# The front of an attention and expert kernel put in order by a greedy list, with sums per half and the scale folded into the joined weights

## The chip, the cores and the metric

The kernel runs on one core of a Trainium2 chip. The metric is the device time of one execution in microseconds (us). The engines are named as in the profile: PE (TensorE, matmuls), PEld (its weight loads), DVE (VectorE), ACT (ScalarE), POOL (GpSimd) and SP (SyncE, which issues nearly all DMAs). Each engine takes its instructions in the order of the program; semaphores let one engine wait for another.

## The reference

Cross attention, then a mixture of eight experts, on 16 batches of 112 tokens with 256 features. The context has 375 rows a batch.

```python
q = layernorm(x) @ Wq + bq;  k = ctx @ Wk + bk;  v = ctx @ Wv + bv
x = x + softmax(q @ k.T / 16) @ v
n = layernorm(x)
cw = softmax(n @ w_router) * softmax(10 * (n @ w_gating));  cw = cw / (sum(cw) + 1e-9)
x = x + sum over e of cw[e] * ((silu(n @ w_gate[e]) * (n @ w_up[e])) @ w_down[e])
```

w_gate and w_up are 8 x 256 x 1024, w_down is 8 x 1024 x 256. All is float32.

## The kernel before, in words

**Attention.** Wq and Wk are joined once into M = Wq Wk^T (turn_weights L190, join_weights L200), the biases into a column r, a row v and a scalar (join_biases L210, join_key_bias L220). Four batches are a group: attn_group (L233) makes the statistics of x on DVE, the power on POOL (L245), the normed x (xn, L251, DVE), its transposes, and qk = M xn + r. attn_batch (L284) is one batch in nine pieces: transposes of ctx and their copies (L293, L296), scores (L300), maximum and two small operations on DVE for the exp's bias (L305 to L309), exp with scale 1/16 (L313, ACT), transposes of p (L318), p times ctx (L327), its split into a high and a low part (L331, L332), projection by Wv in three passes (L337), x1 (L342), a DMA of x1 to the accumulator (L349), statistics of x1 (L353 to L357), the normed x1 (x1n, L360, DVE) and its transposes into x1T (L364, L366).

**Between.** The tokens are two halves of 8 batches. The expert matmuls are done in a seven-product scheme: four blocks of x and of a weight make seven sums each, and seven products replace eight. sums (L378) makes a batch's sums of x on DVE, each cast to a high part xs_hi on ACT (L375) and a low part xs_lo on POOL (L376). route (L394) makes the router's weights of a half.

**Experts.** 128 steps (expert, half, block of features, gate or up); step (L648) runs the seven products (prod, L567; 21 matmuls of 128x448), combines them on DVE (v1, w16, u3, c22, c21, c12) and fills PE in between with the down projection (down_group, L522). Weights come as raw pieces by DMA (L449), are turned into differences tt on POOL (L466 to L469), cast to a high part on ACT (L481) and a low part on POOL (L486). A plan (todo, from L496) says at which step each of this is due.

**Order.** Each engine's order in the front is written out by hand: generators for groups and batches are advanced tick by tick. A batch starts every two ticks, and within a tick the pieces go in a fixed sequence:

```python
    start = [max(0, 2 * b - 2) for b in range(B)]
    def tick(t, order=(3, 4, 2, 5, 6, 0, 1, 8, 7)):
        for s in order:
            for b in range(B):
                if t - start[b] == s == at[b]:
                    batch(b)
```

sums of a batch follow at start + 8 for the later four batches of each half. From tick T_STEP on, what remains of the front waits in a generator (rest), and steps 0 and 1 advance it at fixed points (offer). PSUM banks are taken in turn from a list of eight, of four from T_STEP on. SBUF buffers of the experts serve the front first: seven wide buffers hold x, ctx, qk, x1 and x1T, later the weights.

## Time and profile before

| | us |
|---|---|
| median of 3 runs (1002.86 to 1005.4) | 1004.77 |
| profiled execution | 1002.7 |
| its span, first to last instruction | 1000.9 |
| mean granted PE clock | 0.988 |

Times in the profile are us from the start of the span unless ns is said. In the windows view, PE busy is the time in which PE has a matmul; PEclk is the share of full speed that was granted. A wait line reads: engine, operation and line that waited, what ended the wait, total us, how often, longest.

| group of instructions (line) | count | mean ns |
|---|---|---|
| scores 128x375 on PE (L300) | 64 | 487 |
| exp 112x375 on ACT (L313), and reading its sum | 16 | 576 + 200 |
| normed x on DVE (L251) | 16 | 540 |
| normed x1 on DVE (L360) | 16 | 491 |
| small DVE operations for the exp's bias (L307, L309) | 32 | 214 |
| cast of sums, 128x112, on ACT (L375) | 40 | 280 |
| low part of sums, 128x112, on POOL (L376) | 40 | 450 |
| low part of a block of x, 128x448, on POOL (L376) | 4 | 1162 |
| low part of weights on POOL (L486) | 4 + 4 | 1005, 1322 |

The table holds 5 to 140 us. The ends of matmuls are modelled and overlap, so the time of a piece on PE is best read from start to start.

### The profile page before, as it was taken

The page shows a single profiled execution, that of the slowest core. Times are in us where ns is not written, and L with a number is a line of the kernel's source. Part 1 is how long each engine was busy: PE and PEld are TensorE (multiplying, and loading weights), DVE is VectorE, ACT ScalarE, POOL GpSimd, SP SyncE. Part 2 cuts the span into 40 slices and gives each one's busy share as a digit, 9 for nine tenths or more (in the row PEclk, how much of TensorE's full clock was granted, in tenths as well). Part 3 has the DMA queues.
Part 4 walks back from the last instruction along what each step waited for, and adds up shares of the span by engine and source line. Part 5 has one row for each costly group of instructions (what it writes and reads, how often), then busy time and mean ns, then how long its engine had stood idle before and what let it go on. Part 6 is the DMA issues. An engine that isn't in the chain of part 4 may idle for free.

```text
span 1000.9 us, 16367 instructions
## 1 busy us (share of the span) xinstructions
PE 980.1 (98%) x6052; PEld 911.3 (91%) x6052; DVE 802.8 (80%) x1529; ACT 496.4 (50%) x1036; POOL 419.0 (42%) x548
## 2 busy tenths in 40 slices
PE   8989889999999999999999999999999999999998
PEld 4868779999999999999999999999999999999998
DVE  5886668888878888878887887888887888788786
ACT  4555655445535554445544553555444544455342
POOL 2352765344605552356324460555235632455000
PEclk9999979999999999999999999999999999999999
DMA  9710111001100110011100110011001110010011
GB/s 216 213 30 16 53 32 53 16 28 44 53 1 23 43 43 22 12 42 37 39 11 22 44 54 1 22 44 43 22 11 43 44 32 11 22 43 2 1 37 38
DMA packets 36736, 39.06 MB, mean 39 GB/s; under 512 B 3552, under 2 KB 34656, under 8 KB 36656
## 3 DMA queue, kind: packets, MB, share of 16 engines
q1 hardware_dynamic: 36384, 37.76, 13.1%
q8 instruction: 47, 0.77, 0.3%
q10 hardware_dynamic: 272, 0.26, 0.1%
q14 instruction: 33, 0.27, 0.1%
HBM read 34.34 MB, written 1.84 MB: 36 GB/s over the span
## 4 chain that ended last, share of the span: by engine, by line
PE 93%; DVE 2%; DMA 2%; ACT 1%; POOL 1%; issue 0%; SPq 0%; DVEq 0%
PE pd L539 32%; PE pC L573 16%; PE pA L573 16%; PE pB L573 15%; PE pE L573 8%; PE ps_s L300 2%; PE ps_aT L327 1%; DMA wide<-in_x_dram 1%; PE ps_o L337 1%; PE ps_qk L271 1%; PE ps_lg L401 1%; DMA ctx<-in_ctx_dram 1%; PE ps_cT L293 1%; PE ps_pT L318 1%; ACT xs_hi L375 0%; POOL w L486 0%
## 5 line engine op out<-in xcount | busy, mean ns | idle before, releaser
L539 PE MATMUL pd<-wd,hhi 128*128 128x256 f32 x1792 | 338.6, 280 | 0.0
L539 PEld LDWEIGHTS pd<-wd,hhi 128*128 128x128 f32 x1792 | 310.1, 189 | 15.8
L539 PE MATMUL pd<-wd,hlo 128*128 128x256 f32 x896 | 251.9, 281 | 0.0
L573 PE MATMUL pC<-xs_hi,w 128*128 128x448 f32 x512 | 189.3, 370 | 0.8 <-DVE s_3c L702 0.8
L573 PE MATMUL pA<-xs_hi,w 128*128 128x448 f32 x512 | 188.6, 368 | 0.5 <-ACT v L674 0.4
L573 PE MATMUL pB<-xs_hi,w 128*128 128x448 f32 x512 | 187.9, 367 | 0.0
L539 PEld LDWEIGHTS pd<-wd,hlo 128*128 128x128 f32 x896 | 169.7, 189 | 0.2 <-DVE hlo L626 0.2
L556 POOL TENSOR_TENSOR acc<-acc,y 128x256 f32<-128x256 f32 x45 | 36.1, 831 | 248.4 <-ACT y L555 248.4
L486 POOL TENSOR_TENSOR w<-raw,w 128x384 fp32r<-128x384 f32 x64 | 73.0, 1141 | 136.8 <-ACT w L481 136.8
L674 ACT COPY v<-pA 128x448 f32<-128x448 f32 x128 | 68.1, 532 | 91.2 <-PE pA L573 91.2
L573 PEld LDWEIGHTS pC<-xs_hi,w 128*128 128x128 f32 x512 | 96.8, 189 | 10.0 <-DVE s_3c L702 1.1
L573 PEld LDWEIGHTS pA<-xs_hi,w 128*128 128x128 f32 x512 | 96.8, 189 | 6.0 <-ACT v L674 1.1
L573 PEld LDWEIGHTS pB<-xs_hi,w 128*128 128x128 f32 x512 | 97.2, 190 | 5.5
L573 PE MATMUL pC<-xs_lo,w 128*128 128x448 f32 x256 | 94.1, 368 | 0.0
L573 PE MATMUL pA<-xs_lo,w 128*128 128x448 f32 x256 | 94.1, 368 | 0.0
L573 PE MATMUL pE<-xs_hi,w 128*128 128x448 f32 x256 | 93.7, 366 | 0.0
L573 PE MATMUL pB<-xs_lo,w 128*128 128x448 f32 x256 | 93.3, 364 | 0.0
L486 POOL TENSOR_TENSOR w<-tt,w 128x512 fp32r<-128x512 f32 x64 | 82.9, 1296 | 2.6
L491 POOL TENSOR_TENSOR wd<-rawd,wd 128x512 fp32r<-128x512 f32 x32 | 41.8, 1307 | 72.7 <-ACT wd L490 72.7
L573 PEld LDWEIGHTS pE<-xs_hi,w 128*128 128x128 f32 x256 | 48.2, 188 | 3.9
L573 PEld LDWEIGHTS pB<-xs_lo,w 128*128 128x128 f32 x256 | 48.9, 191 | 1.9
L573 PEld LDWEIGHTS pC<-xs_lo,w 128*128 128x128 f32 x256 | 48.3, 189 | 2.3
(1779 smaller groups left out, 1884.4 us busy)
## 6 DMA issues: line engine op xcount, KB each, us to landing
raw<-in_L_ffn_w_gate_dram SPq DMA_DIRECT2D x32, 256.0 KB, 3.7
raw<-in_L_ffn_w_up_dram SPq DMA_DIRECT2D x32, 256.0 KB, 2.7
rawd<-in_L_ffn_w_down_dram SPq DMA_DIRECT2D x32, 256.0 KB, 2.8
ctx<-in_ctx_dram SPq DMA_DIRECT2D x13, 336.0 KB, 7.3
wide<-in_x_dram SPq DMA_DIRECT2D x4, 448.0 KB, 4.7
out_dram<-acc SPq DMA_DIRECT2D x6, 256.0 KB, 2.2
wide<-in_ctx_dram SPq DMA_DIRECT2D x3, 336.0 KB, 7.0
ctx<-in_ctx_dram SPq DMA_DIRECT2D x13, 39.0 KB
```

What stands on the lines that cost most here:

```text
L271: nc.tensor.matmul(ps, m_sb[:, k, m * P : (m + 1) * P], xnT[:, k, :], start=(k == 0), stop=(k == KC - 1),)
L293: nc.tensor.transpose(ps[:, c * KT : (c + 1) * KT], ct[:, c, k * P : (k + 1) * P], ident[:KT, :KT])
L300: nc.tensor.matmul(sc, qkT[g][:, k, i * TQ : (i + 1) * TQ], ctT[k], start=(k == 0), stop=(k == KC - 1),)
L318: nc.tensor.transpose(ps[:, c, :], p[:, c * KT : (c + 1) * KT], ident[:TQ, :TQ])
L327: nc.tensor.matmul(ps[:, k, :], ct[:, c, k * P : (k + 1) * P], pT[:, c, :], start=(c == 0), stop=(c == NK - 1),)
L337: nc.tensor.matmul(po, aT[:, a, k, :], (wv_hi, wv_lo)[w][:, k, :], start=(k == 0 and s == 0), stop=(k == KC - 1 and s == 2),)
L486: nc.gpsimd.tensor_sub(wts[k][1][:, d], w, f(wts[k][0][:, d]))
L491: nc.gpsimd.tensor_sub(t[:, 1], rawds[q], f(t[:, 0]))
L539: nc.tensor.matmul(pd, hs[a][:, t * P : (t + 1) * P], wds[q][w][:, fi, :], start=(opening and s == 0), stop=(last and s == 2), skip_group_ ...
L556: nc.gpsimd.tensor_add(acc[tt], acc[tt], y)
L573: nc.tensor.matmul(ps, w_[w][:, wi, :], (xs_hi, xs_lo)[a][h][xi], start=(start and s == 0), stop=(stop and s == 2), skip_group_check=True,)
L674: nc.scalar.copy(v1, pa)
```

## The change

The hand-written order goes. Every piece of the front becomes an operation of a list (class Line): engine, cost in us, priority, what it reads, writes and which buffers it takes. run() places them greedily: among the engines it takes the one that can begin first, and on it, of the pieces that could begin within 0.02 us, the one with the lowest priority number (mostly the batch's number). Buffers and PSUM banks come free when all their modelled uses have ended. Then all pieces are emitted in the order of their modelled begin.

```diff
+class Line:
+    LAG = {"PE": 0.2, "SP": 0.1}
...
+                t = max((end[d] + (0.0 if ops[d][0] == eng else self.LAG.get(ops[d][0], 0.1)) for d in deps), default=0.0)
...
+            for eng, c in ready.items():
+                at = max(free.get(eng, 0.0), min(x[0] for x in c))
+                x = min((x for x in c if x[0] <= at + 0.02), key=lambda x: (x[1], x[2]))
+                if best is None or at < best[0]:
+                    best = (at, eng, x)
...
+        for at, n in sorted(line):
+            ops[n][3]()
```

The loads: warm-up matmuls go from 8 to 11; ctx 0 is loaded before the bias rows, x of group 1 before Wv and ctx 2.

```diff
-    WARM = 8
+    WARM = 11
...
+        op("SP", 0.45, 4 * g - 6 if g else -22, lambda: load_x(g), new=(("xg", ("xg", g)),), kb=448)
...
+        op("SP", 0.85, b - 3.5, lambda: load_ctx(b), new=(("ctx", ("ctx", b)),), kb=375)
```

The scale 1/16 goes into M, r and v; the bias of the exp needs one small operation after a negated maximum, where there were two.

```diff
-            nc.scalar.copy(m_sb[:, i, :], ps)
+           lambda: nc.scalar.activation(m_sb[:, i, :], bank(k, [P, D]), AF.Copy, scale=SCALE),
...
-        nc.vector.reduce_max(mx, sc, axis=AX.X)
-        nc.vector.tensor_scalar(mx, mx, cb, None, op0=ALU.add)
-        nc.vector.tensor_scalar(nb, cb, mx, SCALE, op0=ALU.subtract, op1=ALU.mult)
-        nc.scalar.activation(p, sc, AF.Exp, bias=nb, scale=SCALE, accum_out=l)
+           lambda: nc.vector.reduce_max(top[:TQ, col], bank(("sc", b), [TQ, TK]), axis=AX.X, negate=True),
+           lambda: nc.vector.scalar_tensor_tensor(
+               low[:TQ, col], top[:TQ, col], cs[:TQ, col], cs[:TQ, col], op0=ALU.subtract, op1=ALU.add),
+               p(), bank(("sc", b), [TQ, TK]), AF.Exp, bias=low[:TQ, col], accum_out=total[:TQ, col]),
```

The normed x of a group is made on ACT (scale and bias from small columns), but for two of the four batches of group 0. The small per-batch tiles become columns of tiles that hold all batches.

The sums of x are made once a half, on 448 columns. Those of half 0 are in the list. Of half 1 only the two plain blocks X_A11 and X_A12 are; the rest is offered in steps 1 to 3:

```diff
-    def sums(b, eng):
+    def sum_x(h, i):
...
+        for i in (X_A11, X_A12):
+            split(h, i, (6.5, 28)[h], *early(h))
+    for n, i in enumerate((X_S1, X_S2, X_S3, X_S4)):
+        op("DVE", 0.63, 9.5 + 0.1 * n, lambda i=i: sum_x(0, i),
...
+    for i in (X_S2, X_S1, X_S3, X_A22, X_S4):
+        split(0, i, 10.5, *late(0), *([("sx", i)] if i != X_A22 else []))
...
+    def sums_later():
+        for i in (X_S1, X_S2, X_S3, X_S4):
+            sum_x(1, i)
+            yield
+        for i in (X_S2, X_S1, X_S3, X_A22, X_S4):
+            split_hi(1, i)
+            yield
+            split_lo(1, i, V if i in (X_S1, X_S2) else GP)
+            yield
```

The first three weight pieces (EARLY = 3), the first down weights, the whole of step 0 and the first product of step 1 are in the list too, with priorities after all batches. Step 0 takes its temporaries from buffers of the last batches, and its silu waits for every exp, those of both routers among them:

```diff
+    def P1(tag, i, start, stop, reads=(), fresh=False):
+        op("PE", 0.61, 30, lambda: first(tag, i, start, stop),
...
+    tail_s = [("ctT", b, k) for b in range(B - 3, B) for k in range(KC)]
+    P1("A", 1, True, False, fresh=True)
+    op("ACT", 0.54, 30, v1_, reads=(("first", "A"),), writes=("v1",),
+       waits=[("aT", B - 2), ("aTl", B - 2)])
+    P1("B", 6, True, True, fresh=True)
+    w16 = add("w", "v1", "B", "v1", ("first", "B"), waits=tail_s)
+    P1("C", 5, True, False, fresh=True)
+    P1("A", 2, False, True, reads=("v1",))
+    op("ACT", 1.9, 30, silu0, reads=(("first", "A"), "exp", w16), writes=("silu0",))
+    P1("E", 7, True, True, fresh=True)
...
+    op("PE", 0.61, 31, second, reads=(("w", 1), ("xs", 0, X_A11)), new=(("bank", ("second",), BANKS[4:]),))
...
+    line.run()
+    carry["silu01"] = lambda: silu(0, (0, 1), e0["c12"])
-    for n in range(len(steps)):
+    for n in range(1, len(steps)):
+        if n == 1:
+            waiting.append(sums_later())
         step(n)
```

Banks: the last two batches (from their scores on), the router of half 1 and the first product of step 1 may take only the four banks D0 to D3; step 0 takes A, B, C and E:

```diff
+        some = (BANKS[4:],) if b >= B - 2 else ()
...
+           new=(("bank", ("sc", b), *some),))
```

Steps from 2 on are as before.

## The prediction

> **What bounds the kernel now.** I read the page first: is one engine full, and does the chain that ended last stay on it?

> ```profile
> span 1000.9 us, 16367 instructions
> PE 980.1 (98%) x6052; PEld 911.3 (91%) x6052; DVE 802.8 (80%) x1529; ACT 496.4 (50%) x1036; POOL 419.0 (42%) x548
> PE 93%; DVE 2%; DMA 2%; ACT 1%; POOL 1%; issue 0%; SPq 0%; DVEq 0%
> ```

> TensorE (PE) is the bound, so only its idle time and its slow clock can be won back. The change touches the front (attention, until the expert steps run freely). So I cut the span into stages by the windows view:

> ```profile
> core 0: us, PE busy (x) PEld busy (x) DVE busy (x) ACT busy (x) POOL busy (x), PEclk, DMA share, GB/s
> 0.00:7.00 7.00, 3.98 (x12) 1.47 (x13) 2.11 (x9) 1.49 (x2) 0.70 (x6) 1.00 0.67 164
> 7.00:26.00 19.00, 17.16 (x82) 11.91 (x81) 13.43 (x45) 9.85 (x26) 7.00 (x8) 0.91 1.03 237
> 26.00:60.00 34.00, 34.00 (x231) 27.61 (x229) 26.62 (x97) 19.60 (x56) 14.43 (x22) 1.00 0.60 164
> 60.00:81.00 21.00, 16.91 (x119) 14.76 (x117) 15.71 (x56) 10.50 (x37) 11.58 (x23) 0.92 0.06 18
> 81.00:105.00 24.00, 24.00 (x163) 19.62 (x163) 16.03 (x59) 12.58 (x36) 6.55 (x13) 1.00 0.08 21
> 105.00:151.00 46.00, 38.25 (x188) 33.03 (x187) 30.39 (x75) 27.08 (x68) 34.65 (x55) 0.81 0.14 45
> 151.00:200.00 49.00, 49.00 (x303) 46.37 (x304) 41.52 (x69) 24.81 (x49) 19.63 (x25) 1.00 0.11 32
> ```

> The loss of a stage is idle time (length minus PE busy) plus clock (length times one minus PEclk). 7 to 26: 1.8 + 1.7. 60 to 81: 4.1 + 1.7. 105 to 151: 7.8 + 8.7. The others: none. Together 25.8 us, the most that a better order can win; from 151 us on PE is full. The causes are in the waits of PE up to 120 us and, for the end of the front, in PE's timeline:

> ```profile
> PE ps_pT L318 <- ACT p L313: 6.4, 5, 1.9
> PE ps_w L195 <- DMA wn<-in_L_xattn_Wq_dram: 1.8, 1, 1.8
> ```
> ```profile
> 120.27 1.16 PE L337 MATMUL ps_o<-wv_b,aT 128*112 128x256 f32 x6 [1.50 <-ACT aT L331]
> 128.24 0.60 PE L364 MATMUL ps_x1T<-ident,x1n 112*128 112x112 f32 x2 [2.92 <-DVE x1n L360]
> 129.79 5.99 PE L401 MATMUL ps_lg<-wr,wide 128*128 128x16 f32 x28
> ```

> ACT's timeline at 63 us shows the first cause: five casts xs_hi (L375) of one batch's sums stand ahead of the exp p (L313), and PE waits 1.6 us. The same happens at 70 and 108. At the end x1n (L360) of the last batch stands behind other work on DVE. After it the clock is 0.53 from 128 to 142.

> **What the change is worth, part by part.** The sum is made against the profiled execution (1002.7 us, span 1000.9); the median of the runs shown, 1004.77, lies 2.07 above it, and that is added at the end.

> *The list's costs.* Its order is good only if its costs are right. Against the trace: scores 1.33 (two back to back: 1.26 each), aT 1.35 (1.34), pT 0.33 (0.32), qk 1.51 (1.52), ctT copy 0.45 (0.473), exp 0.78 (0.576 + 0.200), split low 1.12 (1.162), weights low 1.02 and 1.31 (1.005, 1.322), batch statistics 0.8 (0.428 + 0.182 + 0.154). All within about 6%, and PE's own are rather high.

> *PE's work does not change.* A batch takes 4.46 us at full clock (92.20 to 96.65 in the timeline), 16 of them 71.4; a group 2 x 0.39 + 2 x 1.52 = 3.8, four 15.3; joined weights 0.9 + 1.75 + 0.87 = 3.5; router 14 x 0.42 = 5.9; step 0 and the next step's first product 24 x 0.205 = 4.9. Sum 101.0.

> *The other engines get lighter.* DVE: 16 scalar operations at 0.214 go with the folded scale (3.4 us); 14 of 16 norms at 0.54 go to ACT (7.6), against 4 small ones. No row shows this norm on ACT: between the 0.37 of a 128x256 copy and the 0.57 of a 128x448 cast I take 0.43, or 6.0 us on an engine that is half idle; the ends are 5.2 and 8.0, both covered. Sums per half: 8 batches x 5 casts of 0.28 become 10 of 0.567 (11.2 to 5.7 on ACT), the low parts 40 x 0.45 = 18 become at most 10 x 1.16 = 11.6, the sums 9.5 become 8 x 0.62 = 5.0; all of these lie beside PE. By the rows the front then needs about 84 us of DVE, 80 of ACT, 52 of POOL under PE's 101: covered, but at over 80% a queue can make PE wait.

> *Start (3.5 lost).* Three more warm-up matmuls at 0.445 end at about 6.1 where 4.75 was, so the gap before the first transposes (released by Wq at 6.58) falls from 1.84 to 0.5; I let nearly all of the clock's 1.7 go. On SP the first ctx now goes ahead of the bias rows and x of group 1 ahead of ctx 2. Chain of batch 0: x lands at 5.05, statistics 2.5, power 1.0, small ones 0.6, norms 0.9, transposes and copies 1.5, qk 3.0 and copy 0.6 give scores at 15.6 to 16.5 (now 18.6). Left: 1.5. Won: **2.0**. If ctx 2 comes late, 1 us of it is gone.

> *Middle (5.8 lost).* The casts get a later priority than the open batches and can run in the slack of ACT, so the wait behind L375 goes. Next in line is DVE. [...] The rows:

> ```profile
> L360 DVE TENSOR_SCALAR x1n<-wide,mvb,rsb x16: 399/406/1250, 34.4 to 127.7; 112x256 f32<-112x256 f32 x16
> L277 DVE CUSTOM_DVE_ANT_0 junk<-xn,mix x16: 416/424/2053, 15.0 to 89.7; 112x256 f32<-112x256 f32 x16
> ```

> Columns: count, shortest/median/longest ns. The lock is there (1.25 and 2.05 us where 0.41 is usual), but seldom: the means, 0.491 and 0.556, lie 0.09 and 0.13 above the medians. By the rows DVE's 84 us already hold this, and the middle keeps 2.0 of loss, most of it from order that doesn't fit to the tenth of a microsecond. [...] I take the row, because these long operations come late in the list. Left: 2.0. Won: **3.8**.

> *End of the front (16.5 lost).* From the last batch's scores to its x1T, by the rows: 1.3 + 0.54 + 0.2 + 0.78, then 0.33 + 0.44, 1.34 + 0.34 + 0.39, 0.75 + 0.48 + 0.76 + 0.56 + 0.41, 0.2 + 0.35, with 14 handovers of about 0.12: 10.9 us, of which PE works 3.9. To fill the other 7.0 PE has the rest of batch 14 (2.6), of 13 (1.0), router products (2.1) and the 24 products (4.9), together 10.6. So it can be filled, but not everywhere: batches 14 and 15 are held to four banks, of which the router's and the next step's product take one each, and step 0 waits for buffers that batches 13 to 15 set free. I leave 2.5 of idle time here.

> *New wait.* Step 0's silu now reads every exp, the router's of half 1 too. After the last x1T copy: two router products and drain 1.0, copy 0.25, maximum and subtraction 0.72, two exps 0.48, table load 1.28, silu 0.55, handovers 0.4: 4.7 us. In step 1 the multiply by that silu heads DVE's queue; behind it stand u3 and c22 (0.62 each), and PE's product into C needs c22. PE has five products meanwhile, to 3.9 us; c22 is there at 4.7 + 3 x 0.62 = 6.6. PE stands 2.7 us. Nothing in the traced order waits so long there (the multiply waited 0.54). In exchange two table loads of 1.28 on ACT are gone, which hid nothing and win nothing.

> *Clock.* [...] Here gaps of 1.63 and 1.92 (62.8 and 69.1) were followed by 0.5 from 72.9 to 76.1, and 1.50 plus 2.92 by 14 us at 0.53. [...] by the rows the 2.7 (and perhaps one before it) cost 1.7 each. I take the rows: 3.0. Left at the end: 2.5 + 2.7 + 3.0 = 8.2. Won: **8.3**.

> *Handed on.* The splits of half 1 that were made in the front (4 sums and 2 low parts on DVE, 6 x 0.62; 5 casts on ACT; 3 low parts on POOL) now lie in steps 1 to 3. A step takes 6.74 and holds 5.3 to 6.0 of DVE (windows from 164.7 to 178.3), so about 0.7 to 1.4 is free in each: 3.7 does not quite fit into three. Between 0 and 3; I take 1.3. POOL's early step holds 1.9 + 2.3 + 0.65 (weight differences, low parts, down weights) = 4.9 of 6.7 and takes its 3.5 over three steps. Copies of x1 to the accumulators (SP, behind each ctx load) and the raw weight loads, which now follow the last of them, land 2.7 to 3.7 us after issue, a whole step before use: nothing. Lost: **1.3**.

> Sum: 2.0 + 3.8 + 8.3 - 1.3 = 12.8. Profiled 1002.7 - 12.8 = 989.9; against the median 992.0.

> **Rivals.**
> A. The list fits as well as the stages with no loss at all: left are 1 at the start, 0.5 in the middle, 4 at the end. Won about 20: **985**. For it: 26 to 60 and 81 to 105 show a full PE under a fixed order. Against it: the silu wait.
> B. Won in front, given back in the steps: DVE in steps 1 to 3 costs the full 3 and the clock falls there once more or stays low as after 128 (up to 7). Won 3 to 7: **1000**.
> C. The list changes the order but its gaps are only elsewhere; every point won at the end is lost to banks: within 3 of before, **1004**.
> D. Slower. The engines keep a fixed order, and DVE, at 84 of 101, takes over as the bound: an x1n or a bias row behind a POOL operation delays a batch, and each such delay reaches PE. The price is what DVE needs beyond 101; it decides from 127 us on (101 plus the 25.8 now lost), that is when DVE's rows stretch 1.5 times. Batches that each lose 1.9 us, say, with the clock falling in between, give **1010**. Against it: means over medians show 6 us of such stops in the whole front, not 42.

> **How the numbers follow.** The sum's own case (won 8 to 17, 988 to 997): 0.50. A: 0.17. B: 0.15. C: 0.06. D: 0.12. A measurement of this kernel can tell about 0.3% (3 us) from no change; so faster 0.82, same 0.06, slower 0.12. For 8 in 10 the range goes to A's 984 below and to B's end, 1001.5, above; outside stay D, most of C and little beyond A.

> **What would show it.** Right: no clock under 1.0 between 7 and 26; PE full from 26 to about 100 with no wait for p behind xs_hi; the router's last products at about 112 rather than 135; a wait of PE for c22 of step 1 of 2 to 3 us; step 2 some 13 us earlier than now; from then on the same 6.74 per step. Wrong: waits of PE for x1n or nb in every batch (D), DVE full in steps 1 to 3 (B), or a PE that stands for a ctx load at the start.

## The result and the profile after

| | before | changed |
|---|---|---|
| median of 20 runs each (us) | 1003.97 (1001.46 to 1007.44) | 1007.69 (1006.48 to 1010.05) |
| ratio, 95% interval | | 1.0039 [1.0029, 1.0048] |
| profiled execution (us) | 1002.7 | 1007.49 |
| span of it (us) | 1000.9 | 1005.7 |
| mean granted PE clock | 0.988 | 0.993 |

The changed kernel is slower by 0.4%, where 992 us were forecast: 15.7 us above the forecast and outside the range. The page after, in the lines that were read first before:

```profile
span 1005.7 us, 16283 instructions
PE 981.5 (98%) x6055; PEld 911.1 (91%) x6055; DVE 807.0 (80%) x1481; ACT 497.9 (50%) x1017; POOL 416.0 (41%) x516
PE 91%; DVE 4%; DMA 2%; issue 1%; POOL 1%; ACT 0%; DVEq 0%; POOLq 0%; ACTq 0%
```

PE is still the bound, but DVE's share of the chain that ended last has doubled, from 2% to 4%. Fewer operations on DVE, and yet more time on the path. The windows view by the same stages, with one row for the steps added:

```profile
core 0: us, PE busy (x) PEld busy (x) DVE busy (x) ACT busy (x) POOL busy (x), PEclk, DMA share, GB/s
0.00:7.00 7.00, 5.47 (x17) 2.15 (x18) 2.21 (x10) 1.68 (x3) 0.70 (x6) 1.00 0.72 214
7.00:26.00 19.00, 17.19 (x93) 12.32 (x92) 13.85 (x52) 13.48 (x34) 9.65 (x11) 1.00 0.93 243
26.00:60.00 34.00, 31.93 (x205) 25.06 (x204) 25.05 (x78) 20.18 (x52) 11.66 (x14) 1.00 0.53 155
60.00:81.00 21.00, 16.35 (x121) 14.31 (x120) 17.48 (x40) 9.85 (x27) 14.78 (x20) 0.92 0.08 23
81.00:105.00 24.00, 21.50 (x142) 18.48 (x141) 15.73 (x42) 13.89 (x38) 10.06 (x13) 0.93 0.12 37
105.00:151.00 46.00, 39.73 (x222) 33.93 (x221) 34.08 (x75) 24.04 (x55) 21.03 (x27) 0.93 0.09 28
151.00:200.00 49.00, 47.76 (x295) 45.07 (x295) 42.31 (x67) 24.23 (x48) 23.13 (x27) 1.00 0.12 34
200.00:900.00 700.00, 700.00 (x4329) 663.23 (x4328) 573.30 (x978) 346.24 (x681) 305.89 (x378) 1.00 0.10 31
```

The start (7 to 26) has its clock back, and the end (105 to 151) is better: PEclk 0.93 instead of 0.81. The stages from 26 to 105, where PE was to be full, now lose idle time in each and clock in two. The last row hides something. The same row of before, in which PE is just as busy:

```profile
200.00:900.00 700.00, 700.00 (x4353) 664.34 (x4352) 577.67 (x985) 350.31 (x690) 307.80 (x381) 1.00 0.10 31
```

The 700 us are full in both, at full clock, and yet hold 24 matmuls fewer in the changed kernel (4329 instead of 4353): each step takes longer without any wait. "PE busy" can't show that; only counts, or starts of equal instructions, can.

To book both kinds of loss I counted, at each time, the elapsed time less the full-speed time of all PE work begun by then (each kind of matmul at its usual start-to-start time, the same in both kernels, the warm-up left out):

| stage, by the prediction's steps | lost before | lost after | won | forecast |
|---|---|---|---|---|
| start, to 26 us | 11.0 | 9.1 | 1.9 | 2.0 |
| middle, 26 to 105 | 5.9 | 12.7 | -6.8 | 3.8 |
| end of the front, 105 to 151 | 17.6 | 11.4 | 6.2 | 8.3 |
| handed on, 151 to 170 | 0.0 | 1.3 | -1.3 | -1.3 |
| steps, 170 to the end | -6.5 | -1.7 | -4.8 | 0 |
| sum | | | -4.8 | 12.8 |

At 170 us the two kernels stand level (34.5 lost in both): the start and the end have paid for the middle. The sum is the difference of the spans (-4.8). (The steps' losses are negative because the assumed matmul times are a little long; only their difference means something. With the median of each kind as its time the column of what was won reads 1.5, -6.4, 6.1, -1.2, -4.8: a stage is good to some 0.5 us.)

The middle's loss has a name. PE's waits between 5 and 155 us, longest first (us in total, times, longest):

```profile
PE ps_xx L950 <- DVE x1n L942: 7.7, 3, 4.5
PE pB L417 <- DVE s_1w L528: 2.7, 1, 2.7
PE ps_cT L846 <- DMA ctx<-in_ctx_dram: 1.2, 2, 1.0
```

The timeline at the longest (start, duration, then the instruction; in brackets the idle time before it and its releaser):

```profile
75.03 3.31 POOL L267 TENSOR_TENSOR xs_lo<-sx,xs_hi 128x448 fp32r<-128x448 f32 x3
75.09 4.49 DVE L942 TENSOR_SCALAR x1n<-wide,mv,rs 112x256 f32<-112x256 f32 x1 [0.44 <-POOL rs L936]
78.31 1.12 POOL L267 TENSOR_TENSOR xs_lo<-wide,xs_hi 128x448 fp32r<-128x448 f32 x1
79.64 0.64 PE L950 MATMUL ps_xx<-ident,x1n 112*128 112x112 f32 x2 [4.54 <-DVE x1n L942]
```

One pass over 112x256, whose median is 0.475 us, took 4.49. It began 0.06 us after a row of four low parts on POOL, and ended 0.15 us after the row did. Shortest, median and longest of the 16 passes, in ns:

```profile
L942 DVE TENSOR_SCALAR x1n<-wide,mv,rs x16: 403/475/4485, 31.1 to 123.4; 112x256 f32<-112x256 f32 x16
```

The second such place:

```profile
100.97 0.99 POOL L322 TENSOR_TENSOR w<-raw,w 128x384 fp32r<-128x384 f32 x1
101.03 3.25 DVE L942 TENSOR_SCALAR x1n<-wide,mv,rs 112x256 f32<-112x256 f32 x1 [0.44 <-POOL rs L936]
101.93 1.25 POOL L322 TENSOR_TENSOR w<-tt,w 128x512 fp32r<-128x512 f32 x1
103.15 0.98 POOL L322 TENSOR_TENSOR w<-raw,w 128x384 fp32r<-128x384 f32 x1
```

Each POOL operation begins before the one ahead has ended (101.93 is before 100.97 + 0.99): there is no gap in the row. (A third, at 52.1, took 2.33 us beside a row of two, and PE waited 0.6 us for it.) The clock was at a half from 77.5 to 84.4 and from 104.8 to 108.3.

A row without a gap in the records does not always hold the pass. In the same trace:

```profile
33.41 2.33 POOL L787 TENSOR_TENSOR wide<-wide,mix 112x256 f32<-112x256 f32 x3
33.47 0.81 DVE L942 TENSOR_SCALAR x1n<-wide,mv,rs 112x256 f32<-112x256 f32 x1 [0.67 <-POOL rs L936]
```

This row is of additions, each 0.72 us or more, and the x1n was through after the first of them (0.81 us); so was the one at 60.8. The experiments below are about rows of subtractions.

### The profile page after: what moved, and what is told of

It reads as the page before. It is cut to its first block, busy times and chain, and to the rows that moved or that the text cites. A ratio compares the mean times of both kernels' runs of the same rounds, so it can differ in the third digit from the quotient of the medians.

```text
span 1005.7 us, 16283 instructions
## 1 busy us (share of the span) xinstructions
PE 981.5 (98%) x6055; PEld 911.1 (91%) x6055; DVE 807.0 (80%) x1481; ACT 497.9 (50%) x1017; POOL 416.0 (41%) x516
## 3 DMA queue, kind: packets, MB, share of 16 engines
q1 hardware_dynamic: 36384, 37.76, 12.7%
HBM read 34.34 MB, written 1.84 MB: 36 GB/s over the span
## 4 chain that ended last, share of the span: by engine, by line
PE 91%; DVE 4%; DMA 2%; issue 1%; POOL 1%; ACT 0%; DVEq 0%; POOLq 0%; ACTq 0%
PE pd L383 31%; PE pC L417 15%; PE pA L417 15%; PE pB L417 15%; PE pE L417 7%; PE ps_aa L892 2%; PE ps_sc L858 2%; DMA ctx<-in_ctx_dram 1%; DVE x1n L942 1%; PE ps_po L907 1%; PE ps_cT L846 1%; PE ps_pp L879 0%; DMA wide<-in_x_dram 0%; PE ps_lg L978 0%; POOL rs L936 0%
## 5 line engine op out<-in xcount | busy, mean ns | idle before, releaser
L331 POOL TENSOR_TENSOR wd<-rawd,wd 128x512 fp32r<-128x512 f32 x32 | 42.1, 1316 | 68.5 <-ACT wd L329 68.4
```

The source lines that it names most:

```text
L331: nc.gpsimd.tensor_sub(wds[q][1], rawds[q], f(wds[q][0]))
```

## Experiments

Theories: (R) the list packs POOL's long operations back to back, and such a row holds an x1n on DVE for its whole length; (L) the lengthened step comes from where the buffers lie, since the eleven small column tiles (1472 bytes a partition; some expectations say twelve) moved the experts' buffers. Rivals: the loss lies in the new order itself (banks, the remainder of half 1 in steps 1 to 3), or one POOL operation is waited for at most. Ratios are to the kernel before, run on the same chip beside it. Its medians there lie between 1003.71 and 1004.97 us, so a difference in us between kernels of different experiments is good to about 1 us. A step's length is the median over a trace. Distances come from the addresses that the program was given.

**The kernel before once more**, unchanged, as a measure of the measurement.

> The kernel before, unchanged, to see how steady its steps are. In the traces at hand a step takes 6.74 us before and 6.79 after, with the same instructions. If that is a matter of the execution (rival theory: each execution draws its own rate), this profile may show any step between 6.73 and 6.80; if it belongs to the kernel, 6.74 again. Time: same as before, ratio 1.000.

1003.96 us, ratio 0.9996 [0.9982, 1.0011]; the step 6.74 us. So 0.3% is well resolved, and the step's length is a property of a program, not of a run.

**Column tiles moved behind the experts' buffers** in the changed kernel (another pool), so that these lie where they lay before.

```diff
-        return cpool.tile([P, *shape], F32, name=name)
+        return spool.tile([P, *shape], F32, tag=name, name=name, bufs=1)
```

> The changed kernel with the instructions in the same order, but its twelve small column tiles (1472 bytes a partition) lie behind the experts' buffers instead of ahead of them, so that those buffers lie where they lay before. Theory 'addresses': a step falls from 6.79 to 6.74 and the time by about 5 us, to 0.999 of before. Theory 'order of the program' or 'each execution its own': the step stays at 6.79, or anywhere, and the time at 1.004 of before.

1003.14 us, ratio 0.999 [0.9975, 1.0005]: 4.6 us less than the changed kernel. The step fell from 6.787 to 6.740 us; the waits for x1n stayed (7.6 us). Every engine's order is the same, so the step's length hangs on placement.

**A tile of 1472 bytes at the front of the pool of constants**, in the kernel before: it moves the constants, the blocks of x and the experts' buffers together.

```diff
+    pad = cpool.tile([P, 368], F32, name="pad")
...
-        lg = spool.tile([P, NTT, 2, E], F32, tag="lg", name=f"lg{h}", bufs=1)
+        lg = pad[:, : NTT * 2 * E].rearrange("p (j s e) -> p j s e", j=NTT, s=2)
```

> The kernel before with 1472 bytes more in the constant pool (the router's small tile is taken from them), so that the experts' buffers lie as in the changed kernel. Theory 'addresses': a step rises from 6.74 to 6.79, the time by about 5 us, ratio 1.005. Otherwise: step 6.74, ratio 1.000.

1003.25 us, ratio 0.9987 [0.9973, 1.0], step 6.740. The absolute addresses changed and the step didn't. The place of the experts' buffers alone, as my expectation had it, is thus not what counts; here the blocks of x moved along with them.

**x1n on ScalarE**, in the changed kernel, at the same place of the list:

```diff
-                t[0], x1(), mv1[:TQ, b, 0:1], rs1[:TQ, col], op0=ALU.subtract, op1=ALU.mult
+                nm1[:TQ, col], mv1[:TQ, b, 0:1], rs1[:TQ, col], -1.0, op0=ALU.mult, op1=ALU.mult
...
+            nc.scalar.activation(t[0], x1(), AF.Identity, bias=nm1[:TQ, col], scale=rs1[:TQ, col])
```

> The changed kernel with its list as it is, but each normed x1 is made on ACT (scale and a bias column from one small DVE operation) at the place where DVE made it. Theory 'lock': DVE's x1n waits for a whole row of POOL operations (4.49 and 3.25 us where 0.41 is usual); with it on ACT the waits of PE for x1n (7.7 us) and most of the slow clock behind them (about 3.4) go: about 10 us less than the changed kernel, 0.994 of before. Rival 'the list's order itself': x1n would come late anyway since it waits for the power on POOL and for ACT's queue: at most 2 us less.

1001.14 us, ratio 0.9963 [0.9954, 0.9973]: 6.5 us less than the changed kernel, where I expected about 10. The waits for x1n fell from 7.7 to 1.9 us (longest 0.8). Idle time from 60 to 105, by the windows: 3.1 + 0.03 instead of 4.65 + 2.5, and no clock below 1.00 there. Step 2 began at 126.7 us instead of 133.8. The step stayed at 6.787: the losses are separate. Of what is missing 1.7 us lie at the end: the clock was at a half for 6.8 us there (from 123.7) instead of 3.4. This speaks for R, but doesn't yet show that the row is the cause.

**An unused tile of 64 bytes behind the constants**, which moves only the experts' buffers: in the kernel before, and in the changed one.

```diff
+    pad = cpool.tile([P, 16], F32, name="pad")
```

> The kernel before with one unused tile of 64 bytes at the end of the constant pool: same instructions, the blocks of x stay where they are, the experts' buffers (weights, hidden blocks) move by 64 bytes. So far a step took 6.74 us where both lie at 64 above a multiple of 128 bytes (before, changed kernel with the small tiles moved) or both at a multiple of 128 (before with 1472 bytes ahead of everything), and 6.787 where x lies at 64 and the experts' buffers at 0 (the changed kernel, twice). Theory 'phase' (the two must share their place modulo 128): step 6.79, time 5 to 6 us more, ratio 1.005. Rival 'where exactly, or what else is in the constant pool': step 6.74, ratio 1.000.

> The changed kernel with one unused tile of 64 bytes at the end of its constant pool: same instructions in the same order, the experts' buffers move by 64 bytes more. Theory 'phase': step 6.74, time as with the small tiles moved, about 1003. Rival 'where exactly': step stays 6.787, time 1007.7.

Before with it: 1002.65 us, ratio 0.9982 [0.9971, 0.9993], step 6.720. Changed with it: 1003.25, ratio 0.999 [0.998, 1.0], step 6.740. The second came as expected; the first went the other way, which refuted my first rule (a period of 128 bytes). What fits all of these is the distance of the experts' buffers from the blocks of x modulo 256: 64 gives 6.787, 128 gives 6.740, 192 gives 6.720.

**Both repairs**: x1n on ScalarE and the columns behind the experts' buffers.

> The changed kernel with x1n on ACT in the same list and the small column tiles behind the experts' buffers. The two gains should add, since one is in the front and one in the steps: 1007.7 - 6.5 - 4.6 = 996.6, ratio 0.992. If the step's length depends on the order of the front, not on addresses, it stays at 1001.

996.81 us, ratio 0.9932 [0.9911, 0.9952]. The gains add.

**The same, with the sums of half 1 begun two offers later**, to take them from in front of step 1's combination.

```diff
     def sums_later():
+        yield
+        yield
```

> The same, and the sums of half 1 begin two offers later in step 1, so that DVE makes w16 of step 1 before them. PE waits 2.6 us for that w16 now; in DVE's queue ahead of it stand the router's last operations (2.0 us) and two sums (1.2 us). Theory 'sums ahead of w16': the wait falls by 1.2 us and with it perhaps the slow clock after it (6.8 us at half, 3.4 us): 1 to 4 us less, 993 to 995.5. Rival, my prediction's own: step 1 waits for silu behind the router's exps, then nothing changes.

997.46 us, ratio 0.9935 [0.9915, 0.9955]: no gain. The wait for s_1w fell from 2.6 to 1.4 us and step 2 began 4 us sooner (125.4), but PE then waited 0.8 us for s_1c and 1.9 for s_4c, and the clock was at a half from 124.0 to 134.2. At step 8 one of the 4 us was left (173.5 against 174.5). DVE owes these sums within three steps; moving them moves the wait.

**Single operations beside rows of 1, 2, 4 and 8 POOL subtractions**, in a small kernel that leaves the whole layer out.

> A kernel of its own (its output is a copy of x; nothing of attention or experts is computed). DVE, or ACT, makes one 112x256 operation that waits for a small POOL power; behind the power stand 0, 1, 2, 4 or 8 POOL subtractions of 128x448 in a row (about 1.1 us each). Theory 'lock for a whole row': a one-input DVE operation from SBUF (as x1n) takes 0.41 us alone and as long as the row lasts with it, about 1.2, 2.3, 4.5 and 9 us. Rival 'one instruction at a time': never more than 0.41 plus one subtraction, 1.5 us, however long the row. With two SBUF inputs the trace of the changed kernel shows 0.76 to 0.88 for a 0.62 us sum beside POOL, so an interleaving: at most one subtraction. From PSUM, and on ACT: no effect, 0.4 us for all.

The groups of DVE (mean ns after the comma):

```profile
L80 DVE TENSOR_SCALAR scalar_none<-xin,mean,r_scalar_none 112x256 f32<-112x256 f32 x3 | 1.2, 412 | 18.8 <-POOL r_scalar_none L69 18.8
...
L80 DVE TENSOR_SCALAR scalar_four<-xin,mean,r_scalar_four 112x256 f32<-112x256 f32 x3 | 3.6, 1208 | 3.7 <-POOL r_scalar_four L69 3.7
```

From 0.41 to 1.21 us, but no more beside four or eight than beside one; with two SBUF inputs 0.485 to 1.340; from PSUM (0.543), for the batch statistics (0.418) and on ScalarE (0.600) nothing. As it stood, this refuted R. But all subtractions of a row wrote one tile, and its timeline gives 4.74 us for four where each works 1.13: there was a gap of about 0.06 us between them, which the changed kernel's rows don't have.

**The same with a tile for each subtraction**, so that none depends on the one before. The tiles also have the type that the kernels use (fp32r), where the first had f32.

> As the first measurement of single operations beside rows of 1, 2, 4 and 8 GpSimd subtractions of 128x448 (it leaves the whole layer out; the output is a copy of x), with one difference: each subtraction of a row writes a tile of its own, in the type that the kernels use, so that none of a row depends on the one before. The theory 'a row without a gap holds VectorE for its whole length': the one-input pass over 112x256 in SBUF takes 1.2 us beside one subtraction, some 2.3 beside two, 4.5 beside four and 9 beside eight, and the pass with two SBUF inputs likewise; from PSUM and on ScalarE no change. The rival 'only the operation under way is waited for, as in the first measurement': 1.2 us whatever the row, and the 4.49 us of the changed kernel have another cause.

```profile
L81 DVE TENSOR_SCALAR scalar_eight<-xin,mean,r_scalar_eight 112x256 f32<-112x256 f32 x3 | 26.4, 8798 | 2.0 <-POOL r_scalar_eight L70 2.0
L81 DVE TENSOR_SCALAR scalar_four<-xin,mean,r_scalar_four 112x256 f32<-112x256 f32 x3 | 13.4, 4460 | 2.0 <-POOL r_scalar_four L70 2.0
L81 DVE TENSOR_SCALAR scalar_two<-xin,mean,r_scalar_two 112x256 f32<-112x256 f32 x3 | 6.9, 2293 | 2.0 <-POOL r_scalar_two L70 2.0
L81 DVE TENSOR_SCALAR scalar_one<-xin,mean,r_scalar_one 112x256 f32<-112x256 f32 x3 | 3.6, 1207 | 2.0 <-POOL r_scalar_one L70 2.0
```

Now the pass waits out the whole row: 1.21, 2.29, 4.46, 8.80 us. The 4.46 beside four is the 4.49 of the changed kernel. The pass with two SBUF inputs behaves alike (8.93 beside eight), and PSUM (0.544 beside eight), statistics (0.417) and ScalarE (the DVE operation that reads its result waited 2.3 us beside four, 2.5 in the first measurement) are again not touched. Two things differ from the first measurement, the gap and the type; the next experiment keeps the type and changes only the gap.

**Gaps in the rows, and nothing else**: x1n stays on DVE; each of the front's 20 low-part subtractions on POOL is followed by a one-column copy that reads its output.

```diff
         eng.tensor_sub(xs_lo[h][i], block_x(h, i), f(xs_hi[h][i]))
+        if eng is nc.gpsimd:
+            eng.tensor_copy(gap, f(xs_lo[h][i])[:, 0:1])
...
             nc.gpsimd.tensor_sub(wts[k][1][:, d], w, f(wts[k][0][:, d]))
+            if k < 4:
+                nc.gpsimd.tensor_copy(gap, f(wts[k][1][:, d])[:, 0, 0:1])
```

> The changed kernel with x1n still on VectorE, and a copy of one column into a scratch column put behind each of the front's 20 subtractions of the low halves on GpSimd (those of x's sums, and those of the weights of the first four gate and up tiles). Each copy reads the subtraction's output, so it must wait for its end and leaves a gap in the row. Nothing else is moved, the step stays at 6.787 us. The theory 'a row without a gap holds VectorE for its whole length' (4.46 us beside four subtractions without a gap, 1.2 beside four with gaps): the x1n at some 75 us takes about 1.2 to 1.7 us instead of 4.49, the one at some 101 us likewise instead of 3.25, TensorE's waits for x1n fall from 15 us to 4 to 8, and the kernel takes 3 to 7 us less than the changed kernel: 1000.5 to 1004.5 us, ratio 0.996 to 1.000 to the kernel before. The rival 'what counts is how much GpSimd works beside it, gap or no gap': x1n stays at 3 to 5 us, and the 20 copies (0.1 to 0.5 us each) make the row longer: 1008 to 1012 us, ratio 1.004 to 1.008.

998.96 us, ratio 0.9948 [0.9931, 0.9966]: 8.7 us less than the changed kernel, by adding 4.3 us of work to POOL; more than I expected. The place that took 4.49:

```profile
74.01 1.12 POOL L268 TENSOR_TENSOR xs_lo<-sx,xs_hi 128x448 fp32r<-128x448 f32 x1
74.07 1.21 DVE L947 TENSOR_SCALAR x1n<-wide,mv,rs 112x256 f32<-112x256 f32 x1 [0.44 <-POOL rs L941]
75.20 0.18 POOL L270 COPY gap<-xs_lo 128x1 f32<-128x1 f32 x1
75.34 1.16 POOL L268 TENSOR_TENSOR xs_lo<-sx,xs_hi 128x448 fp32r<-128x448 f32 x1
75.34 0.41 PE L955 MATMUL ps_xx<-ident,x1n 112*128 112x112 f32 x2 [1.27 <-DVE x1n L947]
```

DVE gets in at the first gap: 1.21 us. PE's waits for x1n fell from 7.7 to 2.0 us. (The 15 us in my expectation was a mistake; the view of the changed kernel has 7.7.) The windows of this kernel for the middle:

```profile
26.00:60.00 34.00, 32.84 (x214) 25.94 (x213) 24.63 (x80) 21.31 (x55) 13.03 (x18) 1.00 0.56 157
60.00:81.00 21.00, 19.63 (x142) 16.43 (x141) 18.08 (x45) 11.87 (x32) 15.87 (x25) 1.00 0.07 20
81.00:105.00 24.00, 23.09 (x166) 19.38 (x164) 16.62 (x50) 15.51 (x43) 14.85 (x25) 1.00 0.19 58
```

Lost from 26 to 105: 1.2 + 1.4 + 0.9 = 3.4 us, all idle; without the gaps, by the same view, 2.1 + 6.3 + 4.2 = 12.6 (about 1 us of it counted twice, where the slow clock lies inside a wait, from 77.5 to 79.6). This decides for R inside the kernel, and as the subtractions still write fp32r, it is the gap and not the type. The repair left the end as it was or worse: the clock was at a half for 6.8 us (from 122.5) instead of 3.4.

**Distances 64 and 192 in other kernels**: 192 bytes behind the constants in the kernel before (distance 64), 128 in the changed kernel and 64 in the twice repaired one (distance 192). The edits are the unused tile, in other sizes.

> The kernel before, with an unused tile of 192 bytes a partition at the end of the const pool: the experts' buffers lie 192 bytes further on, and nothing else is moved. The theory 'distance modulo 256': the length of a step hangs on the distance between the experts' buffers and the blocks of x, modulo 256 bytes; 128 gave 6.74 us, 192 gave 6.72, 64 gave 6.787. Here the distance is 64, so the step becomes 6.787 us and the kernel some 147 x 0.047 = 6.9 us slower than before (ratio 1.006 to 1.007). The rival 'it is a property of the changed list': only the changed kernel and its relatives have had 6.787; the kernel before stays at 6.72 to 6.74, ratio 0.998 to 1.000.

> The changed kernel with two unused tiles of 64 bytes at the end of the const pool: the distance is 192 modulo 256. By 'distance modulo 256' the step is 6.72 us, below the 6.74 of the variant with one such tile, and the kernel takes 147 x 0.067 = 9.8 us less than the changed kernel, less the part that clock windows take back: 998 to 1002 us, ratio 0.994 to 0.998. The rival 'any shift by less than a whole row of buffers helps, or none does so lawfully': 6.74 or 6.787, ratio 0.999 to 1.004.

> The two repairs together at the best distance: x1 normalized by ScalarE, the twelve columns in the pool behind the experts' buffers, and an unused 64-byte tile, so that the distance is 192 modulo 256. By 'distance modulo 256' its step is 6.72 us instead of the 6.74 of the same kernel without the tile (996.8 us): 147 x 0.02 = 2.9 us less, 994 us, ratio 0.990. By the rival, no difference: 996.8 us, ratio 0.993.

| distance modulo 256 | kernels | step, us |
|---|---|---|
| 64 | changed; x1n on ScalarE; with gaps; **before + 192 bytes** | 6.787 each |
| 128 | before; before + 1472 in front; columns moved; changed + 64; both repairs | 6.740 each |
| 192 | before + 64; **changed + 128; both repairs + 64**; (last experiment) | 6.720 each |

The lengths of the bold ones were forecast and came true. Counts of matmuls say the same, here for before + 192 bytes and before + 64 (before itself: 4353):

```profile
200.00:900.00 700.00, 700.00 (x4328) 663.19 (x4327) 573.29 (x979) 346.67 (x681) 308.60 (x380) 1.00 0.10 30
200.00:900.00 700.00, 700.00 (x4362) 668.81 (x4361) 578.38 (x987) 350.56 (x691) 308.93 (x383) 1.00 0.10 31
```

The times: before + 192 bytes 1009.15 us, ratio 1.0043 [1.0029, 1.0057]; changed + 128 bytes 1000.42, ratio 0.9961 [0.9948, 0.9975]; both repairs + 64 bytes 995.11, ratio 0.9902 [0.9889, 0.9915]. The kernel before becomes slower than the change by an unused tile of 192 bytes, and the changed kernel 7.3 us faster by one of 128. The total moves less than I expected for before + 192 (ratio 1.0043 for 1.006 to 1.007) because I multiplied by 147, the total over a step; the steps are 128, and with the ends of experts they average 6.797 against 6.758 us. Within a step it is not one place alone that moves. From 200 to 900 us the mean from start to start, at 64, 128 and 192, is 212, 203 and 205 to 206 ns for the first matmul of a product behind a down projection (4 in a step); 204, 205 and 198 for the last one in front of it (4); 203.3, 203.6 and 201.9 for those between (13); and the 21 of the down projection together take 2.49, 2.48 and 2.51 us. So 64 loses to 128 mostly at the first, and 192 gains at the others.

**Gaps and distance 192 together.**

> Both repairs in one kernel: the changed kernel with the 20 one-column copies that leave gaps in the front's rows of GpSimd subtractions (ratio 0.9948 by themselves), and with the two unused 64-byte tiles that put the experts' buffers at the distance 192 modulo 256 from the blocks of x (ratio 0.9961 where the changed kernel had 1.0039). If the two causes are separate terms, their gains add: the step is 6.72 us instead of 6.787, 147 x 0.067 = 9.8 us, of which 7.3 reached the total before: 989 to 992 us, ratio 0.985 to 0.988. The rival 'they share a cause, or the clock takes one of them back': no better than the better of the two relatives, 995 to 999 us, ratio 0.990 to 0.995.

992.93 us, ratio 0.9892 [0.9877, 0.9908], the fastest kernel here. It missed the expected 989 to 992 by the same factor of 147: the mean step fell from 6.796 to 6.743, times 126 is 6.7 us, and the total fell 6.0. Against the changed kernel it is 14.8 us less; the two repairs alone gave 8.7 and 7.3.

## Why the prediction was wrong, point by point

**The step that failed: the middle, "I take the row".** The forecast weighed the stops of DVE beside POOL (its "lock") by means over medians of the order before (0.09 us per x1n) and left 2.0 us of loss. The runs showed 12.7. The POOL work of that order was mostly low parts of 0.45 us (40 of them), scattered by ticks. The change makes them 128x448, 1.13 us each, and its list, which knows no tie between DVE and POOL, sends them back to back. The reason given ("these long operations come late in the list") does not fit the list: the diff gives the low parts of half 0 the priorities 6.5 and 10.5, among the batches 0 to 15, and four of them ran at 75 us. For x1n those means counted stops of 1.25 us at most, where a row of subtractions without gaps held DVE for all of it (4.46 us for four in the small kernel, 4.49 in the changed one). The line that the prediction shows for junk had a sign of this. Its longest junk, 2.05 us, is longer than any single POOL operation beside it:

```profile
15.01 1.87 POOL L255 TENSOR_TENSOR wide<-wide,mix 112x256 f32<-112x256 f32 x2
16.33 2.05 DVE L277 CUSTOM_DVE_ANT_0 junk<-xn,mix 112x256 f32<-112x256 f32 x1
16.84 1.26 POOL L802 TENSOR_TENSOR wv_b<-wv,wv_b 128x512 fp32r<-128x512 f32 x1
```

It outlasted two operations in a row, the second addition (to 16.88) and the split of Wv (to 18.10). The mean hid this; the longest instance told it.

**Rival D had the mechanism and the wrong price.** It named x1n behind a POOL operation as the way to be slower, and let it decide only when DVE's rows stretch 1.5 times, that is in every batch. DVE's total hardly mattered: two stops of 4.49 and 3.25 us, with PE's queue right behind them, cost 7.0 us of waits (4.54 and 2.50) and about 4 us of half clock (the 4.7 us from 79.6 to 84.4 and 3.4 us from 104.8, each at a half).

**"Steps from 2 on are as before": 0 became -4.8.** This is the second term that failed. Their code was the same and the step was forecast at 6.74. It was 6.787, because the new columns (the experts' buffers moved by 1472 bytes) changed a distance from 128 to 64 modulo 256. 126 steps of 0.037 us (means) make 4.7. The prediction didn't look at this, and no view of the kernel before could have priced it. What makes PE's starts depend on the distance is open: no run separates the blocks of x from the other constants that lie ahead of the experts' buffers, and a distance of 0 wasn't tried.

**Right in size: the start** (1.9 for 2.0): from 7 to 26 us PEclk is 1.00. That is the clock alone. The gap in front of the first transposes fell from 1.8 to 0.3 us as expected, but the idle time from 7 to 26 stayed at 1.8: where PE had waited 1.1 us for p and 0.4 for ctx loads, it now waited 1.2 for ctx. A late ctx load was named in the prediction as a risk.

**Handed on: 1.3 for 1.3, partly by luck.** The window from 151 to 170 holds one wait, in step 4:

```profile
157.41 0.47 PE L417 MATMUL pC<-xs_hi,w 128*128 128x448 f32 x1 [1.24 <-DVE s_4c L551]
```

But the sums were to be made in steps 1 to 3, and these lie in the stage before. There PE waited for DVE as well, 2.7 us for s_1w, 0.8 for s_1c, and 0.7 and 0.6 for hlo, in the changed kernel alone. What was handed on thus cost more than 1.3 us, and the rest is booked under the end of the front.

**End of the front** (6.2 for 8.3): the direction was right. The new wait was right in size, 2.66 us for 2.7, and wrong in cause. PE did not wait for c22 behind the silu but for s_1w, the first combination of step 1. On DVE stood the rest of the router of half 1 (126.99 to 129.0), then two sums of half 1, then s_1w:

```profile
128.27 0.54 ACT L450 ACTIVATE s_0s<-ps_first_A 128x448 f32<-128x448 f32 x1
...
128.95 0.62 DVE L256 TENSOR_TENSOR sx<-wide 128x448 f32<-128x448 f32 x1
129.60 0.62 DVE L256 TENSOR_TENSOR sx<-sx,wide 128x448 f32<-128x448 f32 x1
...
130.15 0.61 DVE L528 TENSOR_TENSOR s_1w<-v,pB 128x448 f32<-128x448 f32 x1
...
130.68 0.61 DVE L540 TENSOR_TENSOR s_0s<-s_0s,ps_second 128x448 f32<-128x448 f32 x1
...
130.81 0.47 PE L417 MATMUL pB<-xs_hi,w 128*128 128x448 f32 x1 [2.66 <-DVE s_1w L528]
...
132.53 0.74 PE L417 MATMUL pC<-xs_hi,w 128*128 128x448 f32 x1 [0.84 <-DVE s_1c L551]
```

The silu was ready in time: its piece was done on ACT at 128.81 (s_0s), and DVE came to the multiply by it only at 130.68. The wait for c22 (s_1c) was there, but of 0.84 us, and for DVE's queue. The sums that were booked under "handed on" for steps 1 to 3 are thus part of the new wait. Of the signs set out in the prediction, the router's last products came at 125.1 us instead of about 112, and step 2 began 1.8 us earlier than before (133.8 for 135.6) instead of 13.

**The clock** was rightly taken by the rows. The wait of 2.50 us was followed by 3.4 us at a half, 1.7 us of loss, and so was the one of 2.66 (with 0.84 more behind it). The length of a wait alone did not decide: with x1n on ScalarE the longest wait between 60 and 105 us, 1.95 (ended at 80.18), came with a clock of 1.00 in that whole stretch; with both repairs the wait for the same copy was 1.9 us and the clock of that stretch 0.96.

**The two missed terms account for the difference.** Middle 10.6 (3.8 to -6.8), steps 4.8, end 2.1, start 0.1: 17.6 us, which is 12.8 + 4.8. With the rows broken and the distance at 192 the kernel takes 992.9 us, where 992.0 was forecast with neither loss. That the two agree so well is partly chance: distance 192 gives more than the 128 which the forecast had assumed, and some stops of x1n remain. Open is what makes a row hold: rows of subtractions held DVE at 52, 75 and 101 us (2.33, 4.49 and 3.25 us), while the additions at 33.4 and 60.8 us, with records that overlap just as much, let it in after the first (0.81 us each).

## What to carry to other kernels

Before packing an order more tightly, ask which engines are tied by something that the order doesn't know: here a DVE pass over 112x256 from SBUF took 4.49 us beside a row of POOL subtractions without gaps and 1.21 beside one with gaps; passes that read PSUM (0.544 us beside eight), and passes on ScalarE (0.600 beside eight with gaps), were not held. Durations from a loose order were no bound for a dense one (x1n at most 1.25 us before, 4.49 after); look at the longest instance of a row, and at what could stand around it. When a kernel spends nearly all its time in one loop, compare the length of that loop first (counts of matmuls, or start to start), since a new tile may move its buffers (here 1472 bytes of columns, 6.740 to 6.787 us a step).
